# A second mixture-of-experts layer put in written order on three engines, started two tiles earlier, with its logits in another pool

## The chip, the cores and the metric

The kernel runs on one core of a Trainium2 chip. The core has a matrix engine (TensorE, PE in the profile, with its weight loads listed apart as PEld), a vector engine (VectorE, DVE), a scalar engine for functions and copies (ScalarE, ACT), a general engine (GpSimd, POOL) and an engine that here only issues transfers (SyncE, SP). Each engine works through its own instructions in order and waits on semaphores for the others. The metric is the time of one execution on the device in microseconds.

## The reference

There are 2708 tokens of 256 features, a 0/1 matrix `adj`, and two layers. Each is an attention over the neighbours in `adj` and then a mixture of eight experts of which a token uses two, each with a residual and a layer norm ahead of it. The change lies in the second layer:

```python
def _L1_gnn_ref(X, A, W_fc, b_fc, w_att, b_att):
    H = X @ W_fc + b_fc
    s_src = H @ w_att[:d]
    s_dst = H @ w_att[d:]
    scores = s_src[:, None] + s_dst[None, :] + b_att
    scores = jnp.where(A > 0, scores, jnp.float32(NEG_INF))
    return jax.nn.softmax(scores, axis=1) @ H

def _L1_ffn_ref(x, gate_w, gate_b, W1, b1, W2, b2):
    logits = xf @ gate_w + gate_b
    probs = jax.nn.softmax(logits, axis=-1)
    top2_vals, top2_idx = jax.lax.top_k(probs, 2)
    ...
        h = jax.nn.gelu(xf @ w1 + bb1, approximate=False)
        y = h @ w2 + bb2
        return (acc + we[:, None] * y, None)

x = x + _L0_gnn_ref(_layernorm(x), adj, ...)
x = x + _L0_ffn_ref(_layernorm(x)[None], ...)[0]
x = x + _L1_gnn_ref(_layernorm(x), adj, ...)
x = x + _L1_ffn_ref(_layernorm(x)[None], ...)[0]
```

The first layer's attention has queries, keys, a masked softmax and an ELU; its experts normalize their input with weights of their own. The hidden width is 1024 in the first layer's experts and 512 in the second's. Everything is float32.

## The kernel before

**Tiles.** Tokens go in 22 tiles of 128, the last with 20 rows (`NT`, `ROWS`, `TAIL`).

**Second attention.** A score is a term of the row plus one of the column, so the row's term cancels in the softmax, and the weight of a neighbour is the exponential of its own score. `values` makes, tile by tile, one product of the normalized tokens with a folded matrix `wfc`: the 256 values, eight columns `W_fc @ gate`, the score, and eight columns for what the residual adds to the gate's logits. ACT takes the exponential of the score and scales the values with it (`e`); DVE reads the eight logit columns from PSUM (L624). `e` is then split in three bfloat16 parts (POOL, DVE, ACT, DVE; L631 to L636). `attend` multiplies the 0/1 mask with these parts. Output tiles come in groups of 6, 6, 4, 3 and 3 (`GROUPS`), and `values` runs within the first group. `evict` copies a group's results out of PSUM and hands each tile to `finish`, which adds the residual, completes the logits and calls `route`.

**`fold_gate`** makes the gate's columns of `wfc` and `bfc_gate`. It is called once, in the second block of the first layer's attention, and issues all its parts there at once.

**Routing.** `route` (L840 on) is a generator in steps: layer norm with its power on POOL (L203), the logits `lg` (L865), the best two on DVE, the exponentials on ACT (L877), the count of rows per expert by two matmuls on PE (L891, L892) that need the running sum `seen`, the destination rows, and two indirect DMAs from POOL that write the token's row into the region of its expert in `disp`. A `Line` holds these generators; `line.step()` advances them, and a new one starts when `line.gap` steps have passed since the one before.

**Slots.** An expert works on blocks of 128 rows, called slots. `place(s0, s1)` works out on DVE which expert and row a slot has; it is called twice, first for the slots of blocks that are surely full (24 of them once 16 tiles are routed, `FULL_AFTER`), by `begin` while attention still runs, and then for the rest when all tiles are routed. The second call also lets SP write eight blocks of empty rows. `fetch_rows` is a transfer issued by SP (L1064), `fetch_weights` an indirect one from POOL (L1049) into one of four ring buffers, and it moves nothing where the buffer already holds that expert. Rows and weights are asked for three slots ahead (`AHEAD`), weights once the down matmuls of the slot that used the buffer are done.

One slot of the second layer is: two transposes (L1088), a copy of the result to `xe` on DVE (L1098), a copy of the bias row on DVE (L1101), the up matmuls (L1108), four gelus on ACT (L1116), the down matmuls (L1124), two DVE instructions for bias and gate weight (L1130, L1131), and an indirect write of the rows to `xd` from POOL (L1135). In the text, `slot(s)` writes up(s) and then down(s-1). The order on the engines is, however, that of the scheduler of the language's compiler, which places each instruction when its inputs are expected to be there. 45 slots always run (`OFTEN`), and then, by branches on a count loaded from the chip, as many more as there are; here two.

**Pools.** SBUF space is taken from pools. A pool opened after another was closed may use the same space, and its first writer then waits for the last readers of the earlier one. `logits` lies in the pool `att1` of the attention, and `xe` in `ffn2`, which is opened when attention has ended. The kept residual `kept` has a pool of its own that stays open.

Of the kernel before, what the change touches and what calls it, by code (L numbers as in the profile page):

```python
# [9 lines left out]
F32 = mybir.dt.float32  # L10
# [4 lines left out]
AF = mybir.ActivationFunctionType  # L15
# [28 lines left out]
GROUPS = [6, 6, 4, 3, 3]  # L44


FULL_AFTER = {16: 24}
SURE = -(-2 * N // P)
CAP = (NT + 1) * P
SLOTS = (2 * N - E) // P + E  # L50
# [10 lines left out]
def adj_ffn_kernel(ctx: ExitStack, tc: tile.TileContext, a: dict, out: bass.AP):  # L61
# [96 lines left out]
    def fold_gate():  # L158
        for c in range(DC):
            junk = small.tile([P, D], F32, name="junk", bufs=1)  # L160
            nc.vector.scalar_tensor_tensor(
                junk, wfc[:, c, :D], 1.0, wdst_b,
                op0=ALU.mult, op1=ALU.mult, accum_out=wfc[:, c, VALUES : VALUES + 1],
            )
        share = routing.tile([P, DC, P], F32, name="gT", bufs=2)
        nc.vector.memset(share[:, 0], 1.0 / D)
        ps = misc.tile([P, GROUP, P], F32, name="misc").rearrange("p g n -> p (g n)")
        for c in range(DC):
            nc.tensor.matmul(
                ps[:, :E], share[:, 0], wg[:, c, :], start=(c == 0), stop=(c == DC - 1)  # L170
            )
        G = wfc[:, :, VALUES + 1 :]
        for c in range(DC):
            nc.vector.tensor_sub(G[:, c], wg[:, c], ps[:, :E])

        def times_gate(dst, src):

            turned = routing.tile([P, DC, P], F32, name="gT", bufs=2)
            to_columns(turned, src, P)
            ps = misc.tile([P, GROUP, P], F32, name="misc").rearrange("p g n -> p (g n)")  # L180
            for c in range(DC):
                nc.tensor.matmul(
                    ps[:, :E], turned[:, c], G[:, c], start=(c == 0), stop=(c == DC - 1)
                )
            nc.vector.tensor_copy(dst, ps[:, :E])

        for c in range(DC):
            times_gate(wfc[:, c, D:VALUES], wfc[:, c, :D])
        times_gate(bfc_gate, bfc_b)


# [98 lines left out]
    def layer0_attention(line):  # L290
        with ExitStack() as scope, ExitStack() as until_last:
# [225 lines left out]
                prepare(t, first[t])  # L517
            g = queries(0)
            late, total, accs = [], None, None
            for b, (b0, nb, ts_) in enumerate(BLOCKS):  # L520
                mT = of_block(b, "mT", [P, NT, nb], FP8)
                nc.gpsimd.memset(mT[:, NT - 1, :], 0.0)
                later_mask = iter(())
                if b + 1 < len(BLOCKS):
                    apart_next = mask_of(b + 1)
                    later_mask = (x for i in range(4) for x in load_mask(b + 1, i, apart_next))
                for k in range(NT):
                    if b == 0:
                        if k + 6 < NT:
                            load_x(k + 6)  # L530
                        if k % 5 == 0 and k < 15:
                            for _ in load_mask(0, k // 5 + 1, apart):
                                pass
                        if k + 4 < NT:
                            prepare(k + 4, norm(k + 4))

                    j = k - (2 if b == last else NT - 1 - GROUP)
                    if 0 <= j < len(ts_):
                        load_x(ts_[j])
                    late.append((b, k, scores(b, k, g, apart, mT)))  # L540
                    if len(late) > LAG:
                        b_, k_, p = late.pop(0)
                        if k_ == 0:
                            accs = [
                                ps_acc.tile([P, D + 1], F32, name="acc") for _ in BLOCKS[b_][2]
                            ]
                        attend(b_, k_, p, accs)
                        if k_ == NT - 1:
                            evict(b_, accs, total)
                    if b == 1 and k == GROUP:  # L550
                        fold_gate()
                    if b == 0 and k == NT - 1:
                        sums = wide.tile([P, DC], F32, name="sums", bufs=1)
                        nc.vector.tensor_reduce(sums, xnT, AX.X, ALU.add)
                        total = all_sum(wide, sums, wv, D, "total0")
                    if k == NT - 6 and b + 1 < len(BLOCKS):
                        g_next = queries(b + 1)
                    if k >= 2:
                        next(later_mask, None)
                    if background and b > 0 and k % 5 == 1 and (b > 1 or k > 10):  # L560
                        background.pop(0)()
                    if b > 0:
                        line.step()
                    if b == last and k == LAG:
                        until_last.close()
                    if b == last and k == LAG + 2:
                        experts0.open()
                        experts0.begin()
                nc.sync.dma_start(neighbours[b][:], mT)
                if b < last:  # L570
                    for _ in later_mask:
                        pass
                    g, apart = g_next, apart_next
# [9 lines left out]
    def layer1_attention(mTs, kept, line):  # L583
        with ExitStack() as scope:
# [1 line left out]
            ps_acc = scope.enter_context(tc.tile_pool(name="acc1", bufs=6, space=PSUM))  # L586
            parts = pool.tile([P, NT - 1, 3, VALUES + 1], BF16, name="parts", bufs=1)

            logits = pool.tile([P, NT, E], F32, name="logits", bufs=1)
            spread_of = pool.tile([P, NT], F32, name="spread_of", bufs=1)  # L590
            e_tail = pool.tile([P, VALUES + 1], F32, name="e_tail", bufs=1)
            sums_of = pool.tile([P, DC, NT], F32, name="sums_of", bufs=1)
# [19 lines left out]
            def values(t, xT):  # L612
                r = P
                ps = misc.tile([P, GROUP, P], F32, name="misc").rearrange("p g n -> p (g n)")
                for c in range(DC):
# [5 lines left out]
                q, weight = ROWS[t], e[:r, VALUES : VALUES + 1]  # L621
                nc.scalar.activation(weight, ps[:r, VALUES : VALUES + 1], AF.Exp)
                nc.scalar.activation(e[:r, :VALUES], ps[:r, :VALUES], AF.Copy, scale=weight)
                nc.vector.scalar_tensor_tensor(  # L624
                    logits[:q, t], ps[:q, VALUES + 1 : VALUES + 1 + E],
                    spread_of[:q, t : t + 1], bfc_gate[:q], op0=ALU.mult, op1=ALU.add,
                )
                if t == NT - 1:
                    return
# [60 lines left out]
            for g, wide in enumerate(GROUPS):  # L690
# [26 lines left out]
                if g == 0:  # L717
                    sums = pool.tile([P, DC], F32, name="sums", bufs=1)
                    nc.vector.tensor_reduce(sums, sums_of, AX.X, ALU.add)
                    total = all_sum(pool, sums, wfc, VALUES, "total1")  # L720
                evict(ts_, accs, total)
                g0 += wide

# [38 lines left out]
    class Experts:  # L762
# [308 lines left out]
        def run(self, line):  # L1071
            with (
                self.scope,
                tc.tile_pool(name="ffn2", bufs=2, side="right") as two,
                tc.tile_pool(name="ps_mm", bufs=2, space=PSUM) as ps_mm,
                tc.tile_pool(name="ps_tp", bufs=2, space=PSUM) as ps_tp,
                tc.tile_pool(name="ps_acc", bufs=2, space=PSUM) as ps_acc,
            ):
                self.slots(two, ps_mm, ps_tp, ps_acc, line)

        def slots(self, two, ps_mm, ps_tp, ps_acc, line):
            hidden, own_norm, xd = self.hidden, self.own_norm, self.xd
            _, hc, w2, b2, b1, ln, row = self.packed_weights

            def up(w, xg):
                tp = ps_tp.tile([P, GROUP, P], F32, name="tp")
                for c in range(DC):
                    nc.tensor.transpose(tp[:, c, :], xg[:, c * P : (c + 1) * P], ident)  # L1088
# [1 line left out]
                if own_norm:  # L1090
                    for c in range(DC):
                        nc.vector.tensor_scalar(
                            xe[:, c, :], tp[:, c, :],
                            w[:, ln + c : ln + c + 1], w[:, ln + DC + c : ln + DC + c + 1],
                            op0=ALU.mult, op1=ALU.add,
                        )
                else:
                    nc.vector.tensor_copy(xe, tp[:, :DC, :])  # L1098

                bias2 = two.tile([P, D], F32, name="bias2")  # L1100
                nc.vector.tensor_copy(bias2, w[:, b2:b1])  # L1101
                hT = two.tile([P, hc, P], F32, name="hT")
                for g in range(0, hc, GROUP):
                    ps = ps_mm.tile([P, GROUP, P], F32, name="mm")
# [42 lines left out]
                    tc.add_to_no_dep_group(self.groups[2], start.ins)  # L1147

            n = FULL_AFTER[self.early]
            line.gap = 1  # L1150
            placed, behind = False, None
            def slot(s):
                nonlocal placed, behind
                w, xg = self.fetched[s]
                hT, bias2 = up(w, xg)
                line.step()

                def fetch():
# [3 lines left out]
                if not placed and (not line.busy() or s + AHEAD == n):  # L1162

                    line.finish()
                    self.place(n, SLOTS)
                    placed = True
                if behind is None:
                    fetch()
                else:
                    down(*behind, fetch)  # L1170
# [3 lines left out]
                    background.pop(0)()  # L1174

            def in_a_row(s0, s1):
                nonlocal behind
                for s in range(s0, s1):
                    slot(s)
                down(*behind, lambda: None)  # L1180
                behind = None

# [23 lines left out]
    packed0 = pack_weights("L0_ffn", 1024, True)  # L1206
    packed1 = pack_weights("L1_ffn", 512, False)
    experts0 = Experts(0, 1024, packed0, wr, br_b, True, xd0, disps[0], 16)
    experts1 = Experts(1, 512, packed1, wg, gb_b, False, xd1, disps[1], 16)

    neighbours = [
        dram.tile([P, NT, nb], FP8, name=f"neighbours{b}") for b, (_, nb, _) in enumerate(BLOCKS)
# [74 lines left out]
```

## Time and profile before

| | us |
|---|---|
| median of 3 runs (1365.86 to 1366.70) | 1366.69 |
| the profiled execution, its own time | 1365.33 |
| its span in the trace | 1363.6 |
| layer 1, values and first attention group | 884 to 962 |
| layer 1, other attention groups | 962 to 1108 |
| first up matmul of the second experts | 1122.39 |
| slot 12, first up matmul | 1176.92 |
| slot 44, first up matmul | 1315.27 |
| slots 45 and 46, first up matmuls | 1322.55, 1328.54 |
| down matmuls of slot 46 end | 1333.09 |

Layer 0 takes the span up to the table's first row. The time after the last down matmuls goes to reading the two rows of every token back and adding them to the residual.

The costliest groups of instructions on the page are the matmuls of the experts in both layers (a group's columns: line, engine, operation, output and inputs with their shapes, count, then busy us and mean ns, then the idle time just before them and its most frequent releaser):

```profile
L1124 PE MATMUL acc<-ring,hT 128*128 128x256 f32 x1096 | 272.4, 385 | 16.7 <-ACT hT L1116 9.4
L1108 PE MATMUL mm<-xe,ring 128*128 128x128 f32 x2192 | 274.9, 280 | 4.4 <-DVE xe L1098 3.4
L1116 ACT ACTIVATE hT<-mm,ring 128x128 f32<-128x128 f32 x548 | 156.4, 369 | 358.6 <-issue 337.5
```

A row's mean mixes both layers, full clock and reduced, since the lines are shared by the two layers. Matmuls overlap in the pipeline, so a row's busy time can be longer than the step from one group to the next; steps are read from the timeline's starts.

### The profile page before, as it was taken

To read this page: it belongs to the slowest core of one execution; us is meant where nothing else is said; L and a number is where in the kernel's file an instruction comes from. 1 tells how busy PE (TensorE), PEld (TensorE's weight loads), DVE (VectorE), ACT (ScalarE), POOL (GpSimd) and SP (SyncE) were. 2 spreads that over 40 slices of the span, in tenths; PEclk is the share of its full clock that TensorE was granted. 3 is DMA by queue.
4 is the path that set the end of the run, shared out by engine and by line. 5 is a ranking of instruction groups with operands and counts; after the bars stand their busy time and mean duration, and the time that the engine had idled before them with its cause. 6 is when DMAs were issued, how large, how long until landed. Compare 5 with 4: busy or idle time off the path is not lost. (4 is left out here: it accounts for less than half of the span.)

```text
span 1363.6 us, 21427 instructions
## 1 busy us (share of the span) xinstructions
PE 1251.6 (92%) x7536; PEld 975.8 (72%) x7536; DVE 581.8 (43%) x2261; ACT 333.5 (24%) x1008; POOL 413.1 (30%) x521
## 2 busy tenths in 40 slices
PE   7999999999999999999999999689999868999980
PEld 4666666666566666999999999567887637888860
DVE  5723743636427255512212222276636564333324
ACT  3222212212112223533333233134100003222220
POOL 5200110110111112533333333341144365544440
PEclk8899999999999999999999999889999879999995
DMA  7701355988928327375678454440010033536447
GB/s 215 248 5 40 117 168 132 257 226 222 251 74 186 98 95 283 73 241 157 183 250 292 118 165 130 108 176 1 1 48 29 30 104 122 176 101 226 156 156 252
DMA packets 106058, 201.39 MB, mean 148 GB/s; under 512 B 25633, under 2 KB 79990, under 8 KB 99418
## 3 DMA queue, kind: packets, MB, share of 16 engines
q1 hardware_dynamic: 75740, 109.41, 28.1%
q0 software_dynamic: 27392, 87.78, 20.3%
q10 hardware_dynamic: 2814, 2.77, 0.6%
q8 instruction: 62, 1.02, 0.3%
q14 instruction: 50, 0.41, 0.1%
HBM read 263.63 MB, written 66.12 MB: 242 GB/s over the span
## 5 line engine op out<-in xcount | busy, mean ns | idle before, releaser
L1124 PE MATMUL acc<-ring,hT 128*128 128x256 f32 x1096 | 272.4, 385 | 16.7 <-ACT hT L1116 9.4
L1108 PEld LDWEIGHTS mm<-xe,ring 128*128 128x128 f32 x2192 | 266.8, 195 | 17.3 <-issue 8.3
L1108 PE MATMUL mm<-xe,ring 128*128 128x128 f32 x2192 | 274.9, 280 | 4.4 <-DVE xe L1098 3.4
L1116 ACT ACTIVATE hT<-mm,ring 128x128 f32<-128x128 f32 x548 | 156.4, 369 | 358.6 <-issue 337.5
L1124 PEld LDWEIGHTS acc<-ring,hT 128*128 128x128 f32 x1096 | 194.3, 191 | 45.5 <-issue 13.2
L429 PE MATMUL s<-g,xnT 128*128 128x512 f32 x420 | 206.4, 607 | 6.0 <-DVE mT L441 6.0
L486 PE MATMUL acc<-v,p 128*128 128x257 f32 (+1 forms) x880 | 209.1, 389 | 0.0
L1130 DVE TENSOR_TENSOR y<-acc,bias 128x256 f32<-128x256 f32 x92 | 39.1, 425 | 323.3 <-PE acc L1124 317.6
L655 PE MATMUL acc<-parts,mT 128*128 128x265 bf16 (+1 forms) x1386 | 173.0, 281 | 0.4 <-DVE raw L682 0.3
L486 PEld LDWEIGHTS acc<-v,p 128*128 128x128 f32 (+1 forms) x880 | 153.0, 190 | 18.0 <-issue 0.8
L1049 POOL DMA_INDIRECT ring<-L_ffn_packed,weight_row x98 | 102.8, 1049 | 206.5 <-issue 92.0
L655 PEld LDWEIGHTS <-mT 128*128 128x128 fp8e4 (+1 forms) x1386 | 132.3, 98 | 45.9 <-issue 18.7
L203 POOL TENSOR_TENSOR ln_rs<-ln_rs,minus_half 128x2 f32<-128x2 f32 x88 | 68.1, 776 | 242.2 <-DVE ln_rs L199 210.9
L441 DVE TENSOR_SCALAR mT<-s 128x512 fp8e4<-128x512 f32 x105 | 72.0, 687 | 138.8 <-ACT p L440 138.7
L909 POOL DMA_INDIRECT disp<-row,to x88 | 87.5, 994 | 137.8 <-DVE to L906 52.8
L429 PEld LDWEIGHTS s<-g,xnT 128*128 128x128 f32 x420 | 76.1, 193 | 53.3 <-issue 42.7
L440 ACT ACTIVATE p<-s 128x512 f32<-128x512 f32 x105 | 62.2, 595 | 168.1 <-PE s L435 167.0
L1142 POOL DMA_INDIRECT xd<-y,xg x45 | 70.7, 1571 | 82.8 <-issue 34.8
L435 PEld LDWEIGHTS <-apart 128*128 128x128 fp8e4 x420 | 32.5, 98 | 60.4 <-issue 60.4
L324 DVE TENSOR_SCALAR apart<-adj 128x677 fp8e4<-128x677 int32 x80 | 40.8, 515 | 47.9 <-DMA adj<-in_adj_dram 47.6
L1135 POOL DMA_INDIRECT xd<-y,xg x47 | 47.2, 1004 | 24.0 <-issue 11.3
L877 ACT ACTIVATE p<-p 128x2 f32<-128x2 f32 (+3 forms) x44 | 9.1, 206 | 163.1 <-DVE p L876 85.2
(227 smaller groups left out, 1126.1 us busy)
## 6 DMA issues: line engine op xcount, KB each, us to landing
adj<-in_adj_dram SPq DMA_DIRECT2D x84, 338.5 KB
L_ffn_packed<-in_L_ffn_W_dram SPq DMA_DIRECT2D x16, 1024.0 KB
xg<-disp SPq DMA_DIRECT2D x98, 129.0 KB
L_ffn_packed<-in_L_ffn_W_dram SPq DMA_DIRECT2D x16, 512.0 KB
neighbours<-mT SPq DMA_DIRECT2D x5, 1408.0 KB
mT<-neighbours SPq DMA_DIRECT2D x5, 1408.0 KB
xin<-in_x_dram SPq DMA_DIRECT2D x42, 128.0 KB
ring<-L_ffn_packed SPq DMA_DIRECT2D x4, 1154.0 KB
```

The source lines that it names most:

```text
L203: nc.gpsimd.tensor_tensor(rs[:r, 1], rs[:r, 0], minus_half[:r], ALU.pow)
L429: nc.tensor.matmul(ps[:kr, :nb], xnT[:, c, k0 : k0 + kr], g[:, c, :nb], start=(c == 0), stop=False,)
L440: nc.scalar.activation(p[:kr, :nb], ps[:kr, :nb], AF.Exp, scale=1.0 / 16.0)
L441: nc.vector.tensor_scalar(mT[:kr, k, :], ps[:kr, :nb], -BIG / 2, None, ALU.is_gt, saturate=False,)
L486: nc.tensor.matmul(accs[j][:r], p[keys, q0 : q0 + r], v[keys, k, :], start=(k == 0), stop=(k == NT - 1),)
L655: nc.tensor.matmul(acc[:r], mT[:, k, j * P : j * P + r], parts[:, k, i], start=(k == 0 and i == 0), stop=False,)
L909: nc.gpsimd.indirect_dma_start(disp[:], bass.IndirectOffsetOnAxis(ap=to[:r, j : j + 1], axis=0), rows2[j][:r], None,)
L1049: nc.gpsimd.indirect_dma_start(w, None, packed[:], bass.IndirectOffsetOnAxis(ap=self.weight_row[:, s : s + 1], axis=0), bounds_check=E * P ...
L1108: nc.tensor.matmul(ps[:, i, :], w[:, c * hidden + f * P : c * hidden + (f + 1) * P], xe[:, c, :], start=(c == 0), stop=(c == DC - 1),)
L1116: nc.scalar.activation(hT[:, f, :], ps[:, i, :], AF.Gelu, bias=w[:, b1 + f : b1 + f + 1])
L1124: nc.tensor.matmul(ps, hT[:, f, :], w[:, w2 + f * D : w2 + (f + 1) * D], start=(f == 0), stop=(f == hc - 1),)
L1142: start = nc.gpsimd.indirect_dma_start(xd[:], at, y, None, bounds_check=N - 1, oob_is_err=False, compute_op=ALU.add)
```

## The change

- `logits` is taken from the pool of `kept`. The part of the last tile is zeroed by POOL.
- In `values`, ACT instead of DVE reads the logits from PSUM and scales them; `bfc_gate` is added to all of them by one DVE instruction after `values` has run for all tiles.
- In the second layer, the slots are written under `manual_schedule` for PE, ACT and DVE: these engines take the instructions in the order of the text. The transposes and `xe` become a function `turned` of their own, called one slot ahead, so that the text's order is up(s), turned(s+1), down(s-1). `xe` and the bias row are copied by ACT instead of DVE.
- The second experts `begin` when 14 tiles are routed instead of 16, with 20 surely full slots instead of 24. `line.gap` in the slots is 3 instead of 1 in the second layer.
- `fold_gate` becomes a generator, advanced at every fourth key tile of the second block, and one memset of it goes to POOL.

```diff
-FULL_AFTER = {16: 24}
+FULL_AFTER = {14: 20, 16: 24}
...
-        nc.vector.memset(share[:, 0], 1.0 / D)
+        nc.gpsimd.memset(share[:, 0], 1.0 / D)
+        yield
...
+            folding = fold_gate()
...
-                    if b == 1 and k == GROUP:
-                        fold_gate()
+                    if b == 1 and k % GROUP == 0:
+                        next(folding, None)
...
-            logits = pool.tile([P, NT, E], F32, name="logits", bufs=1)
+            logits = kept_pool.tile([P, NT, E], F32, name="logits")
+            nc.gpsimd.memset(logits[:, NT - 1], 0.0)
...
-                nc.vector.scalar_tensor_tensor(
-                    logits[:q, t], ps[:q, VALUES + 1 : VALUES + 1 + E],
-                    spread_of[:q, t : t + 1], bfc_gate[:q], op0=ALU.mult, op1=ALU.add,
+                nc.scalar.activation(
+                    logits[:q, t], ps[:q, VALUES + 1 : VALUES + 1 + E], AF.Copy,
+                    scale=spread_of[:q, t : t + 1],
                 )
...
+                    nc.vector.tensor_add(
+                        logits, logits, bfc_gate.unsqueeze(1).to_broadcast([P, NT, E])
+                    )
...
-                self.slots(two, ps_mm, ps_tp, ps_acc, line)
+                with ExitStack() as order:
+                    if not self.own_norm:
+
+                        order.enter_context(tc.manual_schedule(engines={
+                            mybir.EngineType.PE,
+                            mybir.EngineType.Activation,
+                            mybir.EngineType.DVE,
+                        }))
+                    self.slots(two, ps_mm, ps_tp, ps_acc, line)
...
-            def up(w, xg):
+            def turned(s):
+                w, xg = self.fetched[s]
...
-                    nc.vector.tensor_copy(xe, tp[:, :DC, :])
+                    nc.scalar.copy(xe, tp[:, :DC, :])
+                return xe
+
+            def up(w, xe):
 
                 bias2 = two.tile([P, D], F32, name="bias2")
-                nc.vector.tensor_copy(bias2, w[:, b2:b1])
+                (nc.vector.tensor_copy if own_norm else nc.scalar.copy)(bias2, w[:, b2:b1])
...
-            line.gap = 1
-            placed, behind = False, None
-            def slot(s):
-                nonlocal placed, behind
+
+            line.gap = 1 if own_norm else 3
+            placed, behind, xe = False, None, None
+
+            def slot(s, s1):
+                nonlocal placed, behind, xe
                 w, xg = self.fetched[s]
-                hT, bias2 = up(w, xg)
+                if own_norm:
+                    xe = turned(s)
+                hT, bias2 = up(w, xe)
                 line.step()
...
+
+                if s + 1 < s1 and not own_norm:
+                    xe = turned(s + 1)
...
             def in_a_row(s0, s1):
-                nonlocal behind
+                nonlocal behind, xe
+                if not own_norm:
+                    xe = turned(s0)
                 for s in range(s0, s1):
-                    slot(s)
+                    slot(s, s1)
...
-    experts1 = Experts(1, 512, packed1, wg, gb_b, False, xd1, disps[1], 16)
+    experts1 = Experts(1, 512, packed1, wg, gb_b, False, xd1, disps[1], 14)
```

More of the change, by code (lines that the diff above doesn't have):

```diff
@@ L174, in fold_gate @@
             nc.vector.tensor_sub(G[:, c], wg[:, c], ps[:, :E])
+        yield
         def times_gate(dst, src):
@@ L188, in fold_gate @@
             times_gate(wfc[:, c, D:VALUES], wfc[:, c, :D])
+            yield
         times_gate(bfc_gate, bfc_b)
```

## The prediction

> **What bounds the kernel now.** I read the totals first, then a table by stage, then in each stage the waits and the timeline of the engine that is late. The totals (engine, busy us, share of the span, instructions) name TensorE:
>
> ```profile
> PE 1251.6 (92%) x7536; PEld 975.8 (72%) x7536; DVE 581.8 (43%) x2261; ACT 333.5 (24%) x1008; POOL 413.1 (30%) x521
> ```
>
> So a gain can only come from TensorE's 8% of idle time or from a clock below full. The answer by stretch says where they lie. Its columns: stretch, its length, busy us of PE, PEld, DVE, ACT, POOL, granted clock, DMA share, GB/s. The rows are layer 1: values with the first attention group, the other groups, the passage to the experts, slots 0 to 11, slots 12 to 44.
>
> ```profile
> 884.00:962.00 78.00, 69.75 (x453) 53.30 (x454) 56.46 (x211) 30.10 (x87) 23.78 (x42) 0.93 0.24 86
> 962.00:1108.00 146.00, 137.42 (x1146) 106.01 (x1144) 80.79 (x496) 10.78 (x56) 53.05 (x86) 0.96 0.09 30
> 1108.00:1122.00 14.00, 2.58 (x16) 1.46 (x14) 9.08 (x55) 0.68 (x3) 11.25 (x13) 0.58 0.55 179
> 1122.00:1177.00 55.00, 50.73 (x316) 45.56 (x317) 23.73 (x107) 15.40 (x53) 29.98 (x34) 0.92 0.48 164
> 1177.00:1317.00 140.00, 129.57 (x849) 114.89 (x847) 47.90 (x130) 36.61 (x128) 66.80 (x66) 1.00 0.49 160
> ```
>
> The passage is almost empty on PE (2.58 of 14 us); the last row leaves 10.4 us idle at full clock. The passage's timeline (start, us, engine, line, operation, in brackets the idle time before it and its releaser):
>
> ```profile
> 1108.15 0.43 DVE L682 COPY raw<-acc 128x265 f32<-128x265 f32 x1 [1.47 <-PE acc L661]
> ...
> 1110.29 0.66 PE L1088 MATMUL tp<-ident,xg 128*128 128x128 f32 x2 [1.45 <-DMA xg<-disp]
> ...
> 1121.93 0.41 DVE L1098 COPY xe<-tp 128x256 f32<-128x256 f32 x1
> ...
> 1122.39 6.17 PE L1108 MATMUL mm<-xe,ring 128*128 128x128 f32 x32 [0.47 <-DVE xe L1098]
> ```
>
> The token block is transposed by 1110.95, yet its copy xe runs 11 us later, behind the routing of the last tiles on DVE: the last reader of logits (L865) starts at 1121.33, waiting 2.41 us for a POOL power. A steady slot:
>
> ```profile
> 1211.31 1.95 PE L1108 MATMUL mm<-xe,ring 128*128 128x128 f32 x16
> 1213.10 0.38 PE L1088 MATMUL tp<-ident,xg 128*128 128x128 f32 x2
> 1213.35 1.15 ACT L1116 ACTIVATE hT<-mm,ring 128x128 f32<-128x128 f32 x4 [3.14 <-issue]
> 1213.77 1.99 PE L1124 MATMUL acc<-ring,hT 128*128 128x256 f32 x8 [0.29 <-issue]
> ```
>
> The down matmuls of a slot stand right behind its own up matmuls, and so wait for its gelus. When slots are interleaved, as the early ones are, nothing waits:
>
> ```profile
> 1131.25 2.05 PE L1108 MATMUL mm<-xe,ring 128*128 128x128 f32 x16
> 1133.13 1.03 PE L1124 MATMUL acc<-ring,hT 128*128 128x256 f32 x4
> 1134.00 0.38 PE L1088 MATMUL tp<-ident,xg 128*128 128x128 f32 x2
> 1134.22 1.03 PE L1124 MATMUL acc<-ring,hT 128*128 128x256 f32 x4
> 1135.09 1.98 PE L1108 MATMUL mm<-xe,ring 128*128 128x128 f32 x16
> ```
>
> Start to start that is 3.84 us.
>
> **The change part by part.** All sums are against the profiled execution, 1365.33 us (span 1363.6); the median of the runs, 1366.69, stands 1.36 above it.
>
> *1. Front.* With logits in the kept pool, xe no longer needs space that a reader of logits still holds. In the changed order place(0) and the first fetches stand about 131 attention matmuls earlier (1146 took 146 us, so some 17 us), and the first block has landed when attention ends. The last attention matmul ends at 1108.67, and the PSUM copy behind it at about 1109.0. Transpose (0.4), copy (0.4) and semaphores bring the first up matmul to about 1110.0 instead of 1122.39: **-12.4**.
>
> *2. Steady slots, 12 to 44.* From slot 12's first matmul (1176.92) to slot 44's (1315.27) are 32 steps of 4.323. In text order PE has up(s), transpose(s+1), down(s-1): the gelus have a whole slot, and 3.84 is the price. Next late is xe, now on ACT behind the gelus: 2.04 us after the up matmuls' start the gelus begin, 1.15 us they take, a copy takes 0.37 to 0.42, so xe is there at about 3.55, 0.3 before it is needed. DVE loses two copies per slot, of 0.42 and 0.35. 32 x (4.323 - 3.84) = **-15.5**; xe deciding by 0.3 would leave -6.
>
> *3. Lag.* Down matmuls now trail by a slot, and the last must drain before the branch that asks for further slots: **+1.4** (down of slot 43 no longer lies ahead of slot 44).
>
> *4. Early slots, with routing in them.* Beginning at 14 tiles leaves six or seven tiles to be routed between slots, and in text order each of their exponentials stands between gelus on ACT. Before, all had run ahead of the first gelu, so that ACT held one table load in the slots:
>
> ```profile
> L1116 ACT ACT_TABLE_LOAD x1 | 1.3, 1283 | 0.5 <-PE mm L1108 0.5
> ```
>
> After, five slots switch to Exp and back, ten loads more. Ahead of xe one such slot needs load 1.28, Exp 0.40 with its accumulator read, and latencies: xe 3.23 after the up matmuls end instead of 1.89, of which 0.3 were slack, so +1.1 to +1.3. Behind xe the two loads delay the next gelus by 0.9 less slack, and p, late by 0.9, adds as much: about 1.5. Here a rule speaks against the change: the Trainium skill ("ScalarE: Activation LUTs", What ACT_TABLE_LOAD costs) charges about 2.7 us for each switch, load plus drain, and advises finishing one set before the next. By it each of the five slots loses 1.4 to 2.8 more, 7 to 14 in all, and the sum would end at 1344 to 1351. In the row the load takes 1.283 and the first gelu follows it without more than latency, so I take 1.5 each, 7.5, and 0.7 for the last tile's tail. place() for the later slots moves from slots 4-5 to slot 9; its DVE run (n_e at 1148.31 to token_row at 1153.29) holds back one y and the bias copy behind it: +1.0. SP then has eight writes of empty rows (6.8 us at 1149.2) ahead of slot 12's fetch, but four more slots were fetched before: +1.2. Before: 1122.39 to 1176.92 = 54.5, with 8 us of such stalls (steps of 6.18 and 8.37) and a first slot at half clock. After: 12 x 3.84 = 46.1 + 8.2 + 1.0 + 1.2 = 56.5: **+2.0**.
>
> *5. Weights.* A ring buffer is free when its down has ended, now one slot later, so a load (POOL issue to landing 5.7 us, 7.0 to 7.7 where two overlap, 9.0 at worst) has 7.4 us instead of about 13. Seventeen slots load: most still fit, few stick out by 1 to 2. Ends 0 and +6; by the 5.7 row **+1.0**.
>
> *6. Values.* Logits are now read from PSUM by ACT right after e instead of by a DVE instruction, for which PE waits:
>
> ```profile
> PE misc L616 <- DVE logits L624: 6.1, 8, 1.8
> ```
>
> (us, times, longest.) With 0.5 on L215 that is 6.6. ACT pays 22 small copies of some 0.2 us, hidden by its idle time (30 busy of 78). What may be late next is the third engine step there:
>
> ```profile
> ACT parts L633 <- DVE rest L632: 34.8, 21, 3.8
> ```
>
> ACT stands waiting for DVE, and behind it the next e and logits, hence the PSUM buffer. Ends 0 and -7.3; near the row with a third taken back: **-4.5**.
>
> *7. Small ones.* The gate's folding, until now one burst at about 151 us with PE waits of 1.5 and 0.6, is spread over block 1: **-1.5** (0 to -2). One addition of the gate bias to all logits (128x176, like tab's 0.33) before the eviction: **+0.3**. The moved memsets lie on idle POOL: nothing.
>
> Sum: -12.4 - 15.5 + 1.4 + 2.0 + 1.0 - 4.5 - 1.5 + 0.3 = -29.2, so 1336.1 for the profiled execution, and **1337.5** beside the median.
>
> **The rivals.**
> *A: the steady slot stays near 4.2.* ACT now holds xe, bias and gelus in a fixed order; if a wait of one (bias behind the last y, xe behind the gelus) or the landing of weights takes the place of the old wait, part 2 shrinks to -4: 1349. For it: slack of only 0.3. Against: ACT is busy 36.6 of 140 us there, and two copies add 0.8 per slot.
> *B: the front keeps its wait.* If xe still waits for something that the routing holds (a PSUM bank, a DVE result), -12.4 becomes 0 to -3: about 1348. Against: in the built order the first xe waits for nothing past the end of attention.
> *C: slower.* In text order an Exp holds ACT, with gelus and xe behind it, until its p comes from DVE, which waits for a POOL power that queues behind that slot's weight and scatter issues (1.04 and 1.0 us each) and behind the dispatch writes of the tile before. In the passage ACT waited 10.3 us for such a p, and PE stood 3.3 and 4.9 us in attention on the same chain. There is 29 us to lose over five slots: from 5.9 more each (7.4 in all) it decides. At the longest waits, 8.2 per slot, the time is about 1337.5 + 5 x 6.7 = 1371. Against: with two steps per slot and a gap of three, p has about a slot to arrive.
>
> **How the numbers follow.** The forecast with its own spread (1329 to 1345) 0.70; A 0.14, B 0.08, C 0.06, and 0.02 for mixtures that end near 1366. A measurement here can tell about 0.2% (2.7 us) from no change. The range: below, parts 5, 6 and 7 at their best (-1.0, -2.8, -0.5) and Exp slots at half price (-3.7), 1329; above, A, B or the table rule's higher charge, 1352. Faster 0.92, within 0.2% 0.02, slower 0.06.
>
> **Signs.** Part 1: first up matmul near 1110 minus what parts 6 and 7 moved, clock full there; PE's 7.9 us wait for sel gone. Part 2: steps of 3.8 to 3.9, no gap ahead of the down matmuls; xe as releaser would show A. Part 4: eleven table loads in the slots, PE waits of 1 to 2 us at xe or hT in slots 2 to 10; waits of 5 us and more would show C. Part 5: up matmuls waiting for ring's DMA. Part 6: the wait for logits gone, and the stretch from 884 to 962 shorter by 4 to 5; if it stays, ACT's wait for rest has taken the place. A step of 4.2 or Exp slots of 6 us or more would make the prediction wrong.

## The result, and the profile after

The changed kernel takes 1354.36 us (median of 6 runs, 1351.11 to 1357.48), beside 1366.70 for the kernel before: a ratio of 0.9905, interval 0.9886 to 0.9923. It is faster by 12 us, where 29 were forecast. Its profiled execution took 1355.36, with a span of 1353.7 us. Its totals:

```profile
PE 1245.3 (92%) x7536; PEld 973.9 (72%) x7536; DVE 552.6 (41%) x2145; ACT 379.8 (28%) x1134; POOL 415.3 (31%) x523
```

TensorE's share has not moved, so there is still idle time to look for. The stretches of layer 1 (columns as before):

```profile
884.00:962.00 78.00, 70.14 (x455) 53.74 (x456) 53.39 (x191) 32.86 (x108) 24.19 (x43) 0.92 0.25 90
962.00:1109.00 147.00, 137.34 (x1137) 105.53 (x1135) 73.96 (x458) 10.03 (x52) 55.34 (x85) 0.97 0.11 35
1109.00:1112.00 3.00, 2.17 (x13) 0.80 (x11) 0.86 (x2) 0.48 (x2) 0.18 (x1) 1.00 0.10 34
1112.00:1182.00 70.00, 47.40 (x316) 42.17 (x317) 36.63 (x173) 36.71 (x94) 37.71 (x43) 0.93 0.48 158
1182.00:1306.00 124.00, 121.50 (x834) 112.57 (x833) 24.88 (x64) 58.08 (x192) 65.86 (x64) 1.00 0.42 131
```

The passage has shrunk from 14 us to 3, and slots 12 to 44 are full. But slots 0 to 11 now take 70 us with PE busy for 47 of them. The starts and ends of matmuls in the two traces give the sum, stage by stage:

| from, to (us) | before | after | difference | predicted |
|---|---|---|---|---|
| start of the span to the first `values` matmul | 886.42 | 887.90 | +1.5 | -1.5 |
| to the end of the last `values` matmul | 76.58 | 74.60 | -2.0 | -4.5 |
| to the end of the attention's mask matmuls | 144.48 | 147.06 | +2.6 | +0.3 |
| to the first up matmul (front) | 14.92 | 2.76 | -12.2 | -12.4 |
| to slot 12's up matmuls | 54.52 | 70.22 | +15.7 | +2.0 |
| to slot 44's up matmuls | 138.35 | 124.01 | -14.3 | -14.5 |
| to the end of the last down matmul | 17.82 | 16.62 | -1.2 | +1.4 |
| to the end of the span | 30.53 | 30.48 | 0 | 0 |
| sum | 1363.62 | 1353.66 | -10.0 | -29.2 |

The front in the timeline:

```profile
1109.49 1.26 PE L666 MATMUL acc<-e_tail,m_tail 20*128 20x265 f32 x6
...
1111.32 0.41 PE L1105 MATMUL tp<-ident,xg 128*128 128x128 f32 x2 [0.56 <-issue]
1111.90 0.37 ACT L1115 COPY xe<-tp 128x256 f32<-128x256 f32 x1 [1.23 <-PE tp L1105]
...
1112.32 2.05 PE L1128 MATMUL mm<-xe,ring 128*128 128x128 f32 x16 [0.59 <-ACT xe L1115]
```

The copy xe starts 0.2 us after its transposes and waits for no routing. A steady slot:

```profile
1193.74 1.95 PE L1128 MATMUL mm<-xe,ring 128*128 128x128 f32 x16
...
1195.52 0.38 PE L1105 MATMUL tp<-ident,xg 128*128 128x128 f32 x2
1195.74 1.89 PE L1144 MATMUL acc<-ring,hT 128*128 128x256 f32 x8
...
1197.47 1.95 PE L1128 MATMUL mm<-xe,ring 128*128 128x128 f32 x16
```

3.73 from start to start, with no bracket: nothing is waited for. What the early slots wait for (1112 to 1183; total us, times, longest):

```profile
PE mm L1128 <- ACT xe L1115: 11.1, 8, 2.3
PE tp L1105 <- DMA xg<-disp: 9.3, 1, 9.3
PE mm L1128 <- issue: 1.2, 1, 1.2
PE mm L1128 <- ACT p L885: 1.2, 1, 1.2
```

Two things: many short waits for xe, and a single long one for rows. The timeline around the long one:

```profile
1160.88 6.93 SPq L943 DMA_DIRECT2D disp<-nobody  x8
...
1164.29 1.05 POOL L1057 DMA_INDIRECT ring<-L_ffn_packed,weight_row  x1 [1.69 <-issue]
...
1167.53 1.04 POOL L1057 DMA_INDIRECT ring<-L_ffn_packed,weight_row  x1 [0.30 <-ACT xe L1115]
...
1168.91 9.98 SPq L1072 DMA_DIRECT2D xg<-disp  x4
...
1178.74 0.66 PE L1105 MATMUL tp<-ident,xg 128*128 128x128 f32 x2 [9.35 <-DMA xg<-disp]
1179.19 3.51 PE L1144 MATMUL acc<-ring,hT 128*128 128x256 f32 x8
```

SP issues the eight empty-row writes of the second `place`, and only then asks for slot 12's rows. Meanwhile POOL has issued two weight loads. The rows have landed 9.7 us after their request (the last increment of their semaphore is at 1178.60). In the kernel before, the first fetch behind the same eight writes is slot 8's:

```profile
1149.16 6.33 SPq L935 DMA_DIRECT2D disp<-nobody  x8
...
1156.23 7.86 SPq L1064 DMA_DIRECT2D xg<-disp  x5
...
1160.22 0.38 PE L1088 MATMUL tp<-ident,xg 128*128 128x128 f32 x2
```

It landed 2.1 us after its request (1158.36), and the transposes, with no bracket, did not wait for it. In the changed kernel, behind the wait the down matmuls take 3.51 instead of 1.89: the granted clock from 1178.5 to 1182.5 was 0.50.

### The profile page after: what moved, and what is told of

It reads as the page before. It is cut to its first block, busy times and chain, and to the rows that moved or that the text cites. A ratio compares the mean times of both kernels' runs of the same rounds, so it can differ in the third digit from the quotient of the medians.

```text
span 1353.7 us, 21527 instructions
## 1 busy us (share of the span) xinstructions
PE 1245.3 (92%) x7536; PEld 973.9 (72%) x7536; DVE 552.6 (41%) x2145; ACT 379.8 (28%) x1134; POOL 415.3 (31%) x523
## 5 line engine op out<-in xcount | busy, mean ns | idle before, releaser
L1128 PEld LDWEIGHTS mm<-xe,ring 128*128 128x128 f32 x2192 | 264.5, 194 | 33.4 <-ACT xe L1115 14.8
L1144 PE MATMUL acc<-ring,hT 128*128 128x256 f32 x1096 | 267.6, 382 | 3.5 <-ACT hT L1136 3.5
L854 POOL COPY row<-token 128x1 int32<-128x1 int32 (+1 forms) x88 | 17.4, 209 | 104.2 <-DMA disp<-row,to 103.3
```

What stands on the lines that cost most here:

```text
L1128: nc.tensor.matmul(ps[:, i, :], w[:, c * hidden + f * P : c * hidden + (f + 1) * P], xe[:, c, :], start=(c == 0), stop=(c == DC - 1),)
L1144: nc.tensor.matmul(ps, hT[:, f, :], w[:, w2 + f * D : w2 + (f + 1) * D], start=(f == 0), stop=(f == hc - 1),)
```

## The experiments

The kernel before had medians of 1359.8 to 1367.2 us in the sets of runs, which ran on different chips; so ratios to it are compared here, and stages within traces. Each result is the ratio to the kernel before, with its 95% interval in parentheses; 0.001 is 1.4 us. "Steps 3 to 9" is the sum of the seven steps from slot 2 to slot 9; a step is the time from one slot's first up matmul to the next slot's, and seven steps of 3.84 are 26.9. "Slots 0 to 12" is as in the table.

**The changed kernel again, on the chip of three of the kernels below** (`rows_two`, `no_tables`, `no_text_order`). No edit.

> The changed kernel as it is, beside the others on the same chip, so that their differences can be read. Both theories: 0.985 to 0.993 of the kernel before; the transposes of slot 12 wait 8 to 10 us for their rows again.

0.9912 (0.9881 to 0.9942). Slot 12 waited 8.5 us for its rows, its step was 14.44, and steps 3 to 9 were 35.2 (38.2 in the first profile). The result and its largest wait repeat.

**Rows ahead of the writes, for slot 12.**

```diff
                     line.finish()
+                    if not own_norm and s + AHEAD < n:
+                        rows[s + AHEAD] = self.fetch_rows(s + AHEAD)
                     self.place(n, SLOTS)
```

> The changed kernel with the rows of slot 12 asked for ahead of the second place(), so ahead of the eight empty-row writes on SP's queue. Theory: the wait of 9.3 us of the transposes of slot 12 for their rows goes, and its weights (landed at 1171.9 in the changed kernel) are what is late next: slot 12 starts near 1172 instead of 1182.5, 1344 to 1347. Rival, the two weight loads in flight hold the rows of slots 12 and 13 in any order, since they share the DMA engines: gain under 4 us, 1350 to 1354.

0.9881 (0.9863 to 0.99). Slot 12's step is 5.37, but slot 13's is 9.63, since now its request is the first behind the writes. From 1158 to 1183 PE waited for:

```profile
PE tp L1105 <- DMA xg<-disp: 4.1, 1, 4.1
...
PE mm L1128 <- DMA ring<-L_ffn_packed,weight_row: 1.4, 1, 1.4
```

**Rows of slots 12 and 13 ahead.** The same, for two slots.

> The changed kernel with the rows of slots 12 and 13 asked for ahead of the second place(). With slot 12 alone, the wait moved to slot 13 (a step of 9.63 us; rows landed at 1170.0, its weights at 1168.8). Theory: the rows behind the eight empty-row writes are the late thing: steps 11 to 14 together 4 to 6 us shorter than with one slot's rows ahead, 3 to 6 us faster than it. Rival, the weights of slot 13, which land within 1.3 us of the rows, take the place: 0 to 2 us faster.

0.9849 (0.9824 to 0.9874), by the ratios 4 us better than one slot's rows, with intervals that overlap a little. The same stretch:

```profile
PE mm L1128 <- DMA ring<-L_ffn_packed,weight_row: 2.9, 1, 2.9
PE mm L1128 <- ACT xe L1115: 1.6, 1, 1.6
```

No wait for rows is left; the weights of slot 13 follow as what is late next, with a wait of 2.9 us in place of 9.3.

**The writes spread.** The eight writes become closures, two of which are run per slot after `place`; no fetch is moved.

```diff
-                for e in range(E):
+                for e in range(E if self.own_norm else 0):
...
+                for _ in range(2 if placed and not own_norm else 0):
+                    if self.empties:
+                        self.empties.pop(0)()
```

> The changed kernel with the eight empty-row writes of the second place() handed out two per slot, beside the row fetches of slots 12 to 15, instead of eight in one run. Theory: slot 12's rows are late because they stand behind a whole run of writes on one queue: its step falls from 14.4 to 4 to 6 us with no fetch moved, 0.983 to 0.987 of the kernel before. Rival, rows and writes are slow because two weight loads of slots 12 and 13 fill the DMA engines: 0.988 to 0.992.

0.9828 (0.98 to 0.9857): better than the changed kernel by 0.8%, about 11 us, and the lowest ratio of the versions that compute the whole result, though its interval overlaps that of `rows_two`. Slot 12's step is 4.83 instead of 14.4. The request for slot 12's rows is the last of these:

```profile
1164.78 1.34 SPq L951 DMA_DIRECT2D disp<-nobody  x2
1167.01 0.35 SPq L1082 DMA_DIRECT2D xg<-disp  x1
```

No weight load was taken away, and the wait is gone, so the run of writes ahead of the rows is needed for it. But this version also takes the rows out of the way of the loads: the request follows the first write by 2.2 us instead of 8.0, and the rows have landed (1169.15) before the first load's packets begin (1169.54). The same holds for `rows_two`. How the wait divides between the writes and the loads is read from the traces' packets, further down; no run here takes the loads away.

**Beginning at 16 tiles.**

```diff
-    experts1 = Experts(1, 512, packed1, wg, gb_b, False, xd1, disps[1], 14)
+    experts1 = Experts(1, 512, packed1, wg, gb_b, False, xd1, disps[1], 16)
```

> The changed kernel with the second experts beginning at 16 routed tiles (24 sure slots) again. Theory: in the changed kernel place(0) stands in the middle of the attention and PE waits 2.8 us there for seen; beginning at 16 takes this wait out of the attention, and the first slot starts about 1 us later because its rows are fetched later: 1351 to 1354, against 1354.4 for the changed kernel. Rival, the earlier beginning is what lets the slots follow attention at once: first slot 3 to 8 us later, 1357 to 1362.

0.994 (0.9917 to 0.9963), by these ratios 4 to 5 us slower than beginning at 14, with intervals that touch. The stages moved more than that: beside the profile of `after_again`, the attention after `values` took 140.7 instead of 146.6, the front 4.06 instead of 2.76, and slots 0 to 12 76.8 instead of 66.4. Two lines of its timeline show where the first slots lose:

```profile
1101.36 0.66 PE L1105 MATMUL tp<-ident,xg 128*128 128x128 f32 x2 [1.54 <-DMA xg<-disp]
1102.69 3.75 PE L1128 MATMUL mm<-xe,ring 128*128 128x128 f32 x16 [0.67 <-ACT xe L1115]
```

The rows are not there when attention ends, and the first up matmuls take 3.75 instead of 2.05; slot 12 waits 9.9 us for its rows here too. The size was the rival's, the way was not: the first slot did not start later after `values`, it ran slower.

**Only the pool, on the kernel before.**

```diff
-            logits = pool.tile([P, NT, E], F32, name="logits", bufs=1)
+            logits = kept_pool.tile([P, NT, E], F32, name="logits")
```

> The kernel before with logits in the kept residual's pool and nothing else changed. Theory: the first up matmul no longer waits for the last reader of logits, 10 to 12 us earlier, and as the scheduler places the routing beside the slots 2 to 5 of it are given back: 1357 to 1362. Rival, without text order the first slots wait for the routing on DVE and the gain is lost there: 1364 to 1368.

1.004 (1.0026 to 1.0054): no gain. The front did shrink, from 14.92 to 5.12, but slots 0 to 12 grew from 54.5 to 60.1, and the first stage, which differs by up to 8 us between profiles of equal code, was 3.9 longer in this one. In its early slots (1110 to 1180):

```profile
PE acc L1124 <- ACT hT L1116: 3.6, 9, 0.8
PE tp L1088 <- DMA xg<-disp: 3.6, 4, 1.6
PE mm L1108 <- DMA ring<-L_ffn_packed,weight_row: 2.7, 2, 2.4
```

So the pool's wait was real, and behind it stood the rows and weights that only the earlier beginning brings in time, and the routing, which now lies in the slots.

**Without the text order.** `manual_schedule` is left out.

> The changed kernel without the text order (the scheduler places the slots' instructions; xe and bias stay on ACT, turned() one slot ahead in the text). Theory: text order alone makes the steady slots 3.73: without it slots 12 to 44 take 137 to 139 us instead of 124, and the early slots, where the scheduler puts the exponentials ahead, take 58 to 64 instead of 70: 3 to 9 us slower in all. Rival, the copies on ACT and the transposes one slot ahead make the steady slot short: 124 to 128, and the time falls below the changed kernel's.

0.9983 (0.9965 to 1.0001). Slots 12 to 44 took 139.0 us and slots 0 to 12 62.8. In the steady slots PE again waits for its own gelus:

```profile
PE acc L1144 <- ACT hT L1136: 9.7, 19, 0.5
```

The steady gain is that of the text order. Both stages came out as the theory had them, and the loss of 0.7%, some 10 us, is just past its upper end.

**xe on DVE, in text order.** `nc.vector.tensor_copy(xe, ...)` in place of `nc.scalar.copy`.

> The changed kernel with xe copied by DVE again, in text order. Theory: text order gives the steady step of 3.73, whichever engine copies xe: slots 12 to 44 within 1.5 us of 124 to 125.4, and in the early slots the Exps no longer stand ahead of xe but the routing on DVE does: within 4 us of the changed kernel (0.988 to 0.994). Rival, xe on DVE behind y waits for the down matmuls: steady steps of 4.2 and more, 1.00 or above.

0.9894 (0.9859 to 0.993), not to be told from the changed kernel. Slots 12 to 44 took 126.5, with 3.73 in most steps. Which engine copies xe does not matter to the steady slot.

**A Copy for the Exp in the slots.** The gate weights of the tokens routed there are other numbers.

```diff
-            nc.scalar.activation(p[:r, :k], p[:r, :k], AF.Exp, accum_out=den[:r, 0:1])
+            func = AF.Copy if getattr(self, "no_tables", False) else AF.Exp
+            nc.scalar.activation(p[:r, :k], p[:r, :k], func, accum_out=den[:r, 0:1])
```

> The changed kernel with a Copy in place of the Exp of the tiles routed in the slots (same instruction count and accumulator read on ACT, no table load; the gate weights of these tokens are then other numbers, which experts and how many rows are chosen stays). Theory: ten table loads of 1.283 us are what lengthens slots 3 to 9 (11.3 us over 3.84 each): these steps fall by 6 to 10 us together, slots 0 to 12 take 60 to 64 us instead of 70. Rival, the routing's DVE and POOL work in the same order lengthens them, the loads lie in ACT's idle time: less than 3 us.

0.9902 (0.9876 to 0.9928), beside 0.9912. Steps 3 to 9 are 33.4. The groups of ACT between 1108 and 1160 have one table load, and in place of the loads a wait (the last columns are the idle time before the Copy and what ended it):

```profile
L1137 ACT ACT_TABLE_LOAD x1 | 1.3, 1283 | 0.0
L886 ACT ACTIVATE p<-p 128x8 f32<-128x8 f32 (+1 forms) x5 | 1.0, 208 | 12.0 <-DVE p L884 5.4 <-DVE sel L895 4.1 <-DVE hot L889 2.4
```

With the Copy ACT stands there for 12.0 us at five places, so the loads of the changed kernel lay partly in time that ACT would have waited.

**The same on the spread writes.**

> The kernel with the empty-row writes spread (0.983 of the kernel before), and a Copy in place of the Exp of the tiles routed in the slots (the gate weights of these tokens are then other numbers). Theory: of 8 to 12 us of excess in the steps of slots 3 to 9 the ten table loads are 2 to 5: 0.979 to 0.981. Rival, the loads are most of it and the single profile of no_tables hid that: below 0.977. Second rival, they cost nothing beside the waits: 0.982 to 0.984.

0.9818 (0.9794 to 0.9842) beside 0.9828. Steps 3 to 9 are 33.4 again, against 35.2 to 39.3 in the profiles with the loads. By the profiles the ten loads cost 2 to 6 us; by the ratios they can't be told from nothing, and they are not most of the excess.

**Exp as a power on POOL.**

```diff
+            if getattr(self, "no_tables", False):
+                nc.gpsimd.tensor_tensor(p[:r], euler[:r], p[:r], ALU.pow)
+                nc.vector.tensor_reduce(den[:r, 0:1], p[:r, :k], AX.X, ALU.add)
```

> The changed kernel with the exponentials of the tiles routed in the slots taken as a power of e on POOL and summed on DVE, so that ACT keeps one table. Theory: the steps of slots 3 to 9 (together 11.3 us over 3.84 each) are longer because of the ten table loads: 7 to 10 us faster, 1345 to 1348, one ACT_TABLE_LOAD left in the slots. Rival, they are longer because xe and the gelus stand in one order with routing work of DVE and POOL, and the power queues behind POOL's DMA issues: 1352 to 1357.

1.0036 (1.0022 to 1.005): slower than the kernel before, further than the rival had it. Steps 3 to 9 sum to 52.0. The waits of PE and of DVE there:

```profile
PE misc L905 <- DVE sel L901: 16.0, 4, 5.6
```

```profile
DVE den L889 <- POOL p L888: 20.2, 5, 4.9
```

DVE stands at the power's result up to 4.9 us: the power takes 1.68 us on POOL, and at the second tile it began 2.6 us after its input was ready, behind two issues of dispatch writes. PE's count matmul, placed in text order ahead of up matmuls, stands behind DVE. The run takes the loads away and puts a longer chain in their place, so it does not price the loads.

**The Exp half a slot later**, on the version with two slots' rows ahead.

```diff
             yield
+            if late:
+                nc.scalar.activation(p[:r, :k], p[:r, :k], AF.Exp, accum_out=den[:r, 0:1])
```

> The kernel with the rows of slots 12 and 13 ahead (0.985 of the kernel before), and in the slots the Exp written half a slot later, when its p is long there. Theory: without table loads 6.5 of 8.3 us of excess in the steps of slots 3 to 9 stayed, and ACT stood up to 4.1 us at p, so the wait for DVE in text order is the larger part: 3 to 5 us shorter, 0.981 to 0.983. Rival, the loads and the waits overlap, and the load alone then keeps the step at 4.9: 0.984 to 0.986.

0.9849 (0.9816 to 0.9883), no gain; steps 3 to 9 sum to 38.8, beside 37.5 in `rows_two`. ACT no longer waits for p at all in the slots, but it had waited only 1.9 us in `rows_two`. My theory, that ACT's wait for p is the larger part and can be moved out of the way, falls.

**line.gap 1**, on the same version.

> The kernel with the rows of slots 12 and 13 ahead (0.985), with line.gap 1 instead of 3 in the slots, so that tiles are routed two per slot. Theory: two Exps between the gelus of two slots share their table loads, but DVE has two tiles (some 7 us) per slot: steps of 6 to 8 us over four slots instead of 5.1 over seven: 0.983 to 0.987. Rival, each tile in flight adds its own wait for POOL's power to ACT and DVE in turn: steps of 9 us and more, 0.988 to 0.993.

0.9909 (0.9873 to 0.9945), 0.6% worse than `rows_two`. The four slots with routing stepped 9.51, 10.50, 8.75 and 9.93, as the rival had it.

**line.gap 4**, on the spread writes.

> The kernel with the empty-row writes spread (0.983), with line.gap 4 instead of 3 in the slots, so one tile is routed in two slots. Theory: each tile costs its table loads and one wait wherever it stands, so that the excess over 3.73 summed over the slots with routing stays at 9 to 12 us: 0.981 to 0.985. Rival, at gap 3 the tiles still hinder one another as they did at gap 1 (23 us for the same tiles), and more room brings the sum below 8: 0.978 to 0.981.

0.9857 (0.9836 to 0.9878), no better than gap 3 on the spread writes (0.9828). Steps 3 to 9 sum to 38.8, and of the next four three are long (5.47, 5.40, 3.90, 5.47). More room between tiles does not lower the price of a tile. Which of the parts of a routed tile makes up the 6.5 us that stay without loads is open.

## Why the prediction was wrong, point by point

**Front: right.** -12.2 for -12.4. It needed the earlier rows as well as the pool: with the pool alone the front fell by 9.8.

**Steady slots and weights: right.** -14.3 for -14.5. That the sum fits is partly luck. The step came out at 3.73 rather than 3.84, which is 3.5 more over 32 steps, and what was late took back 4.6 rather than 1.0: 4.65, 4.43 and 5.03 to slots 32, 33 and 34, where four loads follow one another, and 4.77 to slot 44. PE waited there 2.0 us in all for weights and 1.0 for rows. Rival A did not happen.

**Early slots: this is the step that failed**, +15.7 for +2.0. Its term "SP then has eight writes of empty rows (6.8 us at 1149.2) ahead of slot 12's fetch, but four more slots were fetched before: +1.2" was mis-sized by a factor of nine: slot 12's step was 15.21 in the one profile and 14.44 in the other, 10.6 to 11.4 over 3.84. This term alone makes some 10 of the 19 us by which the whole sum missed (-10.0 for -29.2).

I had named the queue and counted the issue time of the writes. The four slots more were no reserve, since the slots had moved on as well: the request left SP at 1168.91, 0.5 us before slot 12's transposes were due (1167.34 + 2.05), where the kernel before asked for slot 8's rows 4.0 us ahead of their transposes. With the 2.1 us that a landing took in the kernel before, the wait would have been some 1.6, near the +1.2. The rest is the landing: I had carried the old time over, and it took 9.7 us.

The packets of the two traces show what stood beside it. POOL's loads for slots 12 and 13 were in flight from 1166.0 to 1177.2, and at the request half of the writes were still to be done. Each transfer of SP's queue began there when the one ahead ended, the last write ended at 1175.7, and the rows moved from 1175.7 to 1176.9, 8.0 us after the request. By the same measure, from request to last packet:

| row fetch | us |
|---|---|
| kernel before, behind the eight writes, no load in flight | 1.8 |
| kernel before, nothing ahead in the queue, over 2 us beside a load (7 fetches) | 3.3 to 6.4 |
| changed kernel, nothing ahead in the queue, over 2 us beside a load (5 fetches) | 3.7 to 6.6 |
| changed kernel, slot 12: behind the writes and beside the loads | 8.0 |

So behind the writes, without a load, the fetch was hardly late; beside a load it was late with nothing ahead of it; and with both it was latest. The loads' share is read from these traces alone and not shown by a run. In the kernel before, the writes fell between two loads, of which one ended at 1144.5 and the next began at 1164.2. `rows_two` and `spread_empty` each take the wait away and bring 0.6 to 0.8%.

**The Exp slots, 8.2 us: the size was near, the cause only partly.** Measured were 8.3 and 11.3 over 3.84 in the changed kernel's two profiles. But without these loads 6.5 stay, so the loads are not the price of these slots, and that the size came near was luck. The rule of the Trainium skill ("ScalarE: Activation LUTs", What ACT_TABLE_LOAD costs), some 2.7 us per switch, would by estimate put ten switches at 27 us on ACT; on the path they cost 2 to 6. The groups of ACT show 1.283 for each load, and part of the loads lies in waits:

```profile
L1136 ACT ACT_TABLE_LOAD x6 | 7.7, 1283 | 6.5 <-PE tp L1105 5.9 <-PE mm L1128 0.6
L885 ACT ACT_TABLE_LOAD x5 | 6.4, 1283 | 0.1
```

The second half of the rule's charge, the drain, is not seen. Here the gelus end at 1128.43, and the Exp starts 1.3 us later:

```profile
1127.29 1.14 ACT L1136 ACTIVATE hT<-mm,ring 128x128 f32<-128x128 f32 x4 [1.86 <-PE mm L1128]
1128.45 1.28 ACT L885 ACT_TABLE_LOAD   x1
1129.74 0.21 ACT L885 ACTIVATE p<-p 128x8 f32<-128x8 f32 x1
```

The sum by the rule, 1344 to 1351, lay nearer to the 1354 measured, but not for its reason: what was missing sat at slot 12.

Rival C's mechanism exists: in `gap_one`, with steps of 9 to 10, ACT waited 14.6 us for the p of the tiles in flight. At gap 3 with Exp on ACT it stayed below its break-even; ACT's wait for p was 1.1 us in the first profile.

**place() in the attention: left out.** I let the earlier beginning bring rows in time and gave it no cost. PE meets the count of `seen` in the middle of a group:

```profile
1086.01 0.17 PE L930 MATMUL misc<-seen,ones 128*128 128x8 bf16 x1 [2.78 <-DVE seen L908]
```

This wait is new, but it is not the whole +2.6 of that stage: PE's waits for `seen` there were 8.2 us before and 6.5 + 2.8 after, and its busy time rose from 135.9 to 137.4; why is open. The other profiles with `place` in the attention show 1.2 to 5.3 us for this wait. `begin16` moves it out, and loses more at the first slots.

**place() behind slot 9, +1.0: measured 1.7.** The step from slot 10 to 11 is 5.53 in this profile, 1.7 over 3.84, with PE waiting 1.64 for xe behind the bias copy.

**Values: -2.0 in this profile, -2.2 to -3.3 in the others with this code, for -4.5.** The wait for logits fell from 6.6 to 1.5; new ones came, one of them for the chain that I had named as late next:

```profile
PE misc L621 <- ACT logits L629: 1.5, 5, 0.3
PE acc L660 <- POOL parts L635: 1.3, 1, 1.3
```

**Gate folding: no gain that is seen.** The wait of 1.5 is gone. From the 90th to the 240th score matmul the kernel before took 161.4 us (167.8 in `pool_only`), and the fourteen profiles with the folding spread out took 160.4 to 165.1: in the later part of the stretch DVE waits for adjacency rows, up to 8.6 us at once, at a DMA share of 1.03, so that an earlier arrival there probably brings nothing; this was not tried by itself. The stage as a whole, from the start of the span to the first `values` matmul, ends between 883.6 and 891.8 in the profiles with the folding, so neither the -1.5 forecast nor the +1.5 of the table can be told from noise.

**Lag: -1.2 for +1.4.** The drain is there, but the step from slot 44 to 45 shrank from 7.28 to 6.21 all the same; its cause wasn't tried.

## What to carry to other kernels

When a step moves, look up what else will be in flight at its new time: a latency from the old place holds only beside the old neighbours. Count what lies ahead on a DMA queue, and what runs beside it, up to its landing, not only its issue. Text order on an engine is worth most where nothing irregular stands in it; each irregular chain written into it (routing, place) puts its own latency on every engine of the chain.

## What the runs showed of the hardware

Of the eight writes (128 rows of 1032 bytes each), the four ahead of the weight loads took 0.5 us each from first to last packet. Of the four beside the loads (1.18 MB each), two took 3.4 and 3.6 us and the others 0.5 and 0.8, and they ended 5.5 to 8.2 us after their issue instead of 0.7 to 1.4. In `after_again` the longest took 2.9. I had not expected a factor of up to seven. A row fetch with nothing ahead of it on its queue took 1.6 us from request to last packet without a load (the median of 28 in the changed kernel's profile) and 3.7 to 6.6 beside one. The wait of 9.35 us also cost 1.6 us after its end, by the half clock of the next down matmuls (3.51 for 1.89).
